# A fused transformer block on one core: fewer bands of the depthwise convolution on TensorE, more of its products by DMA, and a newly computed order

## The chip, the core and the metric

The kernel runs on one core of a Trainium2 chip. The core has five engines with a queue of instructions each: PE (TensorE, matmuls; its weight loads are listed as PEld), DVE (VectorE), ACT (ScalarE), POOL (GpSimd) and SP (SyncE, which here only issues transfers), and 16 DMA engines that move data. An engine runs its queue in order; between engines, semaphores tell when a result is there. The metric is the device time of one execution in microseconds (us). All data are float32.

## The reference

The input is x of shape 16 x 128 x 96 x 96 (images, channels, rows, columns). One block of an image-restoration transformer is computed: layer norm over the channels, attention between the channels within 8 heads, a residual sum, a second layer norm, a feed-forward part, and a residual sum.

```python
x = x + attn_out                      # attention of layernorm(x, ln1)
xn2 = layernorm(x, ln2)               # over the 128 channels
h1 = einsum('bchw,oc->bohw', xn2, w_in)          # 128 -> 512 channels
h2 = depthwise 3x3 convolution of h1, zero padding, w_dw   # each of 512 channels by itself
h3 = gelu(h2)
x = x + einsum('bchw,oc->bohw', h3, w_out)       # 512 -> 128 channels
```

The change concerns the depthwise convolution, h1 to h2: for each of the 512 channels nine products with shifted images, added up.

## The kernel before

**Tiling.** Channels lie on the 128 partitions. An image is cut into 8 bands of 12 rows (`BR`, 1152 pixels), 128 bands in all (`NG`), and a band into three strips of 4 rows (384 pixels). The 512 hidden channels are four blocks of 128 (n = 0 to 3). So the convolution consists of 128 x 4 pieces (g, n), a band and a block of channels.

**Two ways to compute a piece.** `conv_job` does it with all engines: PE makes h1 of the band from the normalized image (`hidden`, L907), ACT copies it out of PE's accumulators into an SBUF image with a border (`kept`, L912), and then the nine products are shared out. All weights are divided by that of the middle tap (`UNIT`), which then needs no multiplication. DVE computes the first tap with the middle tap added (L925), and each further tap as one instruction, multiply by the channel's weight and add in place (`tap`, L931). Some taps are not computed by DVE: ACT multiplies the shifted image by its weight into a product buffer `pr` (`product`, L920), and a DMA that accumulates adds it up (`add_products`, L941, issued by POOL): the second product of the piece into the first one's buffer (pr<-pr), and the first one's buffer into h3 when DVE is done with its taps (h<-pr). Two taps go this way in every piece (`DMA_TAPS`), and a third one where `third` (L948) holds. Such a piece has one more `pr<-pr` transfer and one tap fewer on DVE. Then ACT applies GELU in place (L945).

`by_matmuls` does a piece of block 3 on PE alone: it takes the composition of w_in and one tap's weights as nine 128 x 128 matrices (`comp`), and accumulates nine matmuls on each strip of the normalized image, 27 for the band (L991); every float32 matmul shows as two passes. GELU then reads the accumulators (L1001). Such a piece needs no h1, no taps, no products and no DMA. `by_pe(g)` (L1041) says which bands have it: counted from the end, k = NG - 1 - g, those of `PE_LAST` among the last eight, and of the others those with k % `PE_OF` in `PE_BANDS`.

`ffn_out` (L1009) multiplies h3 by w_out, four matmuls on each strip (L1018), DVE adds the result to x (L1025), and SP stores the band (L1029). The two norms of every image run beside the convolution of other bands: transposes on PE (L615, L720), statistics on DVE (L622), variance and power on POOL (L629, L633), scaling on ACT (L669, L673), and a Gram matrix on PE (L683). x comes in by SP (L552), and is added to the attention's result by an accumulating DMA that POOL issues (L584).

**The order.** No engine's queue is written by hand. Every step is an `op` of a `Plan` with an engine, a cost in ns, a place, and the buffers that it reads and writes. `Plan.order` (L104) plays the whole program through with these costs: a free engine takes, of the steps whose inputs are ready and whose buffers are free, the one with the lowest place; the steps are then issued in the order of their planned starts. A place is the number of the job plus the kind's offset from the table `AT`. The costs come from `t_mm`, `t_dve`, `t_act`, `t_copy` (L375 and after) and from constants: `T_ADD` for the time that an accumulating transfer occupies the DMA engines, `T_MOVE` for a plain one. Buffers are counted in the plan too: five product buffers (`PR_BUFS`), ten h3 buffers, six and two of x, three of transposed strips, four accumulator banks for matmul results.

Of the kernel before, what the change touches and what calls it, by code (L numbers as in the profile page):

```python
# [17 lines left out]
UR = 4  # L18
BR = 12
PE_CHUNK = 3  # L20
PE_BANDS = (0,)
PE_OF = 2
PE_LAST = (0, 1, 2, 4, 5, 7)
TINY = 1e-20
UNIT_MIN = 1e-18
# [2 lines left out]
FIRST_TAP, THIRD_TAP = 7, 1  # L28
TOP_FIRST, TOP_THIRD = 7, 8
END_FIRST, END_THIRD = 1, 0  # L30
THIRD, THIRD_OF, THIRD_CHUNK = (0, 1, 2), 3, 1
PART, Z_PARTS = 24, 6
QT, QB = 4, 1
H_BANKS = 4
X1_BUFS, XB_BUFS, PR_BUFS, H3_BUFS, ZT_BUFS = 2, 6, 5, 10, 3
IN_TURN = ("tr", "h3", "pr", "xb", "x1")
AT = dict(
    load_w=-0.7, weights=56.25, zeros=-91.75, load_a=-171.6, forth_a=-13.8, stats_a=-13.35, variance_a=472.9,
    power_a=393.55, scaled_a=100.7, gram=-0.95, back_a=-54.2, place_a=177.7, attention=-168.4, mix=-35.75,
    residual=220.5, mixed=-116.4, add_x=-284.15, forth_b=-10.05, stats_b=-175.75, variance_b=89.4,  # L40
    power_b=-306.7, shift_b=-89.65, scaled_b=147.3, back_b=-5.05, place_b=36.3, halo=257.25, hidden=4.1,
    kept=-157.6, products=108.95, add_last=-2.05, tap=5.45, add_first=-115.65, gelu=233, conv=3.9, conv_gelu=5,
    out=7.4, add=-85.8, store=312.6, mix_0=-83.1, residual_0=398.2, mixed_0=-274.7, add_x_0=-395.85,
    gram_0=56.85, forth_a_0=-241.65, forth_b_0=-12.45, stats_a_0=-45.05, stats_b_0=-53.25, scaled_a_0=38.7,
    scaled_b_0=263.2, back_a_0=-243.25, back_b_0=-126.9, place_a_0=-340.95, place_b_0=-9.4, shift_b_0=-42.6,
    late=7.15,
)
STEP = dict(scaled=0.3, hidden=0.1, products=0.5, tap=0.166, conv=1.6, conv_tap=0.03, out=0.8, out_part=0.05)
SLACK = 300
# [3 lines left out]
T_START = 2300  # L53
T_VARIANCE = 420
T_POWER = 1000
T_ADD, T_MOVE = 3060, 1640


class Plan:
# [14 lines left out]
    def op(self, engine, ns, place, work, reads, writes, result, own=None, dma=0, two=False):  # L74

        k = len(self.ops)  # L80
        needs = {}
        for t in reads:
            if t in self.writer:
                needs[self.writer[t]] = True
        for t in writes:
            if t in self.writer:
                needs[self.writer[t]] = True
            for r in self.readers.get(t, ()):
                needs[r] = True
        for t in reads:  # L90
            self.readers.setdefault(t, []).append(k)
        new = []
        for t in writes:
            self.writer[t], self.readers[t] = k, []
            if t[0] in self.free and t[:2] not in self.users and t[:2] not in new:
                new.append(t[:2])
        for t in {t[:2]: None for t in (*reads, *writes)}:
            if t[0] in self.free:
                self.users.setdefault(t, []).append(k)
                needs[self.users[t][0]] = True  # L100
        needs.pop(k, None)
        self.ops.append((engine, ns, place, work, list(needs), new, result, own or result, dma, two))
# [111 lines left out]
def tile_restormer_block(  # L214
# [30 lines left out]
    UT = UR * W  # L245
    TPU = UT // P
# [26 lines left out]
    ones = const.tile([P, 1], F32, name="ones")  # L273
# [79 lines left out]
    def x_unit(of, i, u):  # L353
# [5 lines left out]
        tr=2, bk=1, h=H_BANKS, g=1, batch=4, zT=ZT_BUFS, x1=X1_BUFS, xb=XB_BUFS, pr=PR_BUFS, h3=H3_BUFS  # L359
# [3 lines left out]
    def at(kind, place, i=1):  # L363
        return place + AT[kind if i else kind + "_0"]

    def bank(key, n=4 * P):

        return banks[plan.slot["h", key]][:, :n]
# [4 lines left out]


    def t_mm(n):  # L375
        return 2 * max(110, 0.84 * n)

    def t_dve(n):
        return 100 + 1.067 * n

    def t_act(n, scalars=0):
        return 95 + 93 * scalars + 0.832 * n
# [1 line left out]
    def t_copy(n):  # L384
        return 40 + 0.832 * n

    def pe(ns, p, f, r, w):
        op("PE", ns, p, f, r, w, ns + 200 + SLACK, ns)
# [150 lines left out]
    def x_key(i, b, second):  # L539

        return "xb" if second or i == 0 and b < XB_BUFS else "x1"
# [14 lines left out]
    def norm(i, second, place_of):  # L556

        name = f"{'b' if second else 'a'}{i}"
        ab = "_b" if second else "_a"
        zTs = {}  # L560

        def xtok(u):
            return (x_key(i, u // UPB, second), (i, u // UPB), u % UPB)
# [34 lines left out]
        def pixels(s, m):  # L598
# [8 lines left out]
            def forth(q):  # L607
                if early:
                    d["pT", q] = bank((name, q)).rearrange("p (t c) -> p t c", c=P)
                else:  # L610
                    d["pT", q] = p_tr.tile([P, QT, P], F32, tag="tr", name=f"pT_{name}_{q}")
                for k in range(QT):
                    b, j = divmod(q * QT + k, TPB)
                    xt = (xbs if x_key(i, b, second) == "xb" else x1s)[i, b]
                    nc.tensor.transpose(d["pT", q][:, k, :], xt[:, j * P : (j + 1) * P], ident)  # L615
# [62 lines left out]
            def gram(q):  # L678
                if q == 0:
                    grams[i] = p_g.tile([P, 4 * P], F32, tag="g", name=f"g_{i}")  # L680
                for k in range(QT):
                    zt = zTs[q][:, k, :]
                    nc.tensor.matmul(  # L683
                        grams[i][:, : P + 1], lhsT=zt[:, :P], rhs=zt,
                        start=(q == 0 and k == 0), stop=(q == NU * TPU // QT - 1 and k == QT - 1),
                    )

            trs, bt = [(key_, (name, q)) for q in qs], ("batch", (name, m))
            for q, tr in zip(qs, trs):
                units = {t // TPU: None for t in range(q * QT, (q + 1) * QT)}  # L690
                pe(110 * QT, at("forth" + ab, s, i), lambda q=q: forth(q), [xtok(u) for u in units], [tr])
            for j in range(QB * QT // 2):
                dve(341, at("stats" + ab, s, i), lambda j=j: stats(j), [trs[2 * j // QT]], [bt])
            op("POOL", T_VARIANCE, at("variance" + ab, s), variance, [], [bt], T_VARIANCE + 33 + SLACK + 200)
# [3 lines left out]
            for h, (q, tr) in enumerate(zip(qs, trs)):  # L698
                zt, sh = zt_of(q), s + STEP["scaled"] * h
                if by_dve:  # L700
                    if apart and q % 2 == 0:
                        both = [(*zt_of(k), j) for k in (q, q + 1) for j in range(2)]
                        op("POOL", 200, at("zeros", sh), lambda q=q: zT(q), [], both, 300)
                    dve(by_dve * 240, at("scaled" + ab, sh, i), lambda q=q: also_scaled(q), [tr, bt], [(*zt, 0)])
                act((QT - by_dve) * (343 if second else 250), at("scaled" + ab, sh, i), lambda q=q: scaled(q), [tr, bt], [(*zt, 1)])
                if not second:
                    pe(QT * 220, at("gram", sh, i), lambda q=q: gram(q), [(*zt, 0), (*zt, 1), ("w", "ones")], [("g", i)])

        def zt_of(q):
            return ("h3", ("zT", q // 2), q % 2) if i == 0 and not second else ("zT", (name, q))  # L710

        def channels(s, u):

            d = {}

            def back():
                d["pB"] = p_bk.tile([P, UT], F32, tag="bk", name=f"pB_{name}_{u}")
                for j in range(TPU):
                    q, k = divmod(u * TPU + j, QT)
                    nc.tensor.transpose(d["pB"][:, j * P : (j + 1) * P], zTs[q][:, k, :P], ident)  # L720

            def place():
                if second:
                    nc.scalar.activation(interior(i, u), rows(d["pB"]), AF.Identity, bias=b2)
                else:
                    nc.scalar.copy(interior(i, u), rows(d["pB"]))

            def place_row(k, r, row):
                to = window(xns[k], r, 1, 1)
                nc.scalar.activation(to, rows(d["pB"])[:, row : row + 1, :], AF.Identity, bias=b2)  # L730

            copies = []
            if second and u % UPP == 0 and u > 0:
                copies.append((part_of(i, u * UR - 1)[0], PART + 1, 0, UPP))
            if second and u % UPP == UPP - 1 and u < NU - 1:
                copies.append((part_of(i, (u + 1) * UR)[0], 0, UR - 1, -1))

            pb = ("bk", (name, u))
            quads = {(u * TPU + j) // QT: None for j in range(TPU)}
            pe(110 * TPU, at("back" + ab, s, i), back, [(*zt_of(q), k) for q in quads for k in range(2)], [pb])  # L740
            act(t_act(UT, 1) - 43 if second else t_copy(UT), at("place" + ab, s, i), place, [pb, ("w", "shift")] if second else [pb], [z_unit(i, u)])
            for k, r, row, of in copies:
                act(225, at("place" + ab, s, i), lambda k=k, r=r, row=row: place_row(k, r, row), [pb, ("w", "shift")], [("z", k, of)])
# [7 lines left out]
        u = 0  # L751
# [135 lines left out]
    def conv_job(j, g, n):  # L887

        i, b = divmod(g, NB)
# [55 lines left out]
            nc.scalar.activation(h3, h3, AF.Gelu)  # L945

        last = j == len(jobs) - 1
        third = n == THIRD_CHUNK and g % THIRD_OF in THIRD  # L948
        ahead, also = (TOP_FIRST, TOP_THIRD) if b == 0 else (END_FIRST, END_THIRD) if b == NB - 1 else (FIRST_TAP, THIRD_TAP)
        dma_taps = () if last else (*DMA_TAPS, also) if third else DMA_TAPS  # L950
        left = [ahead, *(t for t in range(9) if t not in (ahead, UNIT, *dma_taps))]
# [89 lines left out]
    def by_pe(g):  # L1041
        k = NG - 1 - g
        return k in PE_LAST if k < NB else k % PE_OF in PE_BANDS

# [58 lines left out]
```

## Time and profile before

| | |
|---|---|
| three runs | 4160.88, 4160.81, 4159.0 us; median 4160.81 |
| the profiled execution | 4157.91 us, of which its span (first to last instruction) is 4156.2 |
| granted PE clock, mean | 0.998 of full speed |
| PE busy | 4116.1 us, 99% |
| DVE busy | 4023.1 us, 97% |
| ACT busy | 3673.4 us, 88% |
| POOL busy | 2466.3 us, 59% |
| DMA engines, queue of POOL and queue of SP | 83.4% and 10.2% of the span |

Busy time is the time in which an engine has at least one instruction running. Instructions of one engine overlap a little, so the durations of a group add up to more than the engine's time. In the lists of groups a line reads: source line, engine, operation, written tile <- read tiles, shape, count | busy time of the group in us, mean duration of one in ns | idle time of the engine just before them, and what ended it. A list of stretches has, for each window in us from the span's start, the busy time of every engine with its number of instructions, the granted PE clock, the DMA engines' mean busy share and what they moved. The share can be slightly over 1, since two packets on one DMA engine can overlap in the records.

### The profile page before, as it was taken

What the parts mean: (1) busy time and instruction counts of PE and PEld (TensorE: products, weight loads), DVE (VectorE), ACT (ScalarE), POOL (GpSimd) and SP (SyncE); (2) the same over time, 40 slices, a digit from 0 to 9 for tenths busy, and PEclk for the clock granted to TensorE, in tenths of its full rate; (3) what the DMA queues carried; (4) which work ended last, traced back from release to release, by engine and by line L of the source; (5) the groups of instructions that cost most, each with busy time, mean ns of one, the idle gap of its engine ahead of it and who ended that gap; (6) DMA issues with size and microseconds to landing.
All of it is one profiled execution on the core that took longest, in us unless ns stands there. A gap on an engine that the chain in (4) does not pass through costs nothing.

```text
span 4156.2 us, 52372 instructions
## 1 busy us (share of the span) xinstructions
PE 4116.1 (99%) x17457; PEld 2679.0 (64%) x17457; DVE 4023.1 (97%) x4676; ACT 3673.4 (88%) x6971; POOL 2466.3 (59%) x2347
## 2 busy tenths in 40 slices
PE   8999999999999999999999999999999999999999
PEld 7666666666666666666666666666666666666565
DVE  7999999999999999999999999999999999999998
ACT  5999998999989888998999989888898998989885
POOL 4667565565656657566465656656557565665442
PEclk9999999999999999999999999999999999999999
DMA  3999999999999989999999999999999999999997
GB/s 94 195 203 212 195 214 203 208 206 197 212 202 208 201 189 212 204 208 203 195 217 189 210 213 193 213 196 202 207 197 211 204 206 196 191 211 190 193 195 171
DMA packets 203934, 827.63 MB, mean 199 GB/s; under 512 B 23568, under 2 KB 24976, under 8 KB 203664
## 3 DMA queue, kind: packets, MB, share of 16 engines
q0 software_dynamic: 164160, 672.47, 83.4%
q1 hardware_dynamic: 38256, 151.73, 10.2%
q8 instruction: 138, 2.26, 0.2%
q14 instruction: 132, 1.08, 0.1%
q10 hardware_dynamic: 1248, 0.09, 0.0%
HBM read 148.26 MB, written 75.50 MB: 54 GB/s over the span
## 4 chain that ended last, share of the span: by engine, by line
PE 84%; ACT 7%; DVE 5%; DMA 2%; issue 1%; POOL 1%; POOLq 0%; ACTq 0%; DVEq 0%
PE h L991 22%; PE h L1018 21%; PE h L907 18%; PE g L683 5%; PE h L572 5%; DVE h L931 3%; PE pB_a L720 3%; PE pT_b L615 3%; PE pT_a L615 2%; PE pB_b L720 2%; ACT pr L920 2%; DMA pr<-pr 1%; ACT zT L673 1%; DMA h<-pr 1%; ACT h L912 1%
## 5 line engine op out<-in xcount | busy, mean ns | idle before, releaser
L931 DVE SCALAR_TENSOR_TENSOR h<-h,ratio,h 128x1140 f32<-128x1140 f32 (+2 forms) x2104 | 2856.9, 1379 | 5.3
L920 ACT ACTIVATE pr<-h,ratio 128x1152 f32<-128x1152 f32 x1018 | 1310.4, 1295 | 69.1 <-DMA h<-pr 41.1
L991 PE MATMUL h<-xn,comp 128*128 128x380 f32 (+1 forms) x3564 | 1261.9, 481 | 4.3 <-ACT h L912 3.9
L1018 PE MATMUL h<-h,woutT 128*128 128x384 f32 x3072 | 1134.1, 488 | 6.2 <-ACT h L945 4.9
L907 PE MATMUL h<-xn,winT 128*128 128x384 f32 (+1 forms) x2676 | 1045.3, 494 | 4.3 <-ACT h L912 2.9
L991 PEld LDWEIGHTS h<-xn,comp 128*128 128x128 f32 x3564 | 645.9, 189 | 380.4 <-issue 8.2
L941 POOL DMA_DIRECT2D pr<-pr x573 | 557.9, 988 | 507.5 <-ACT pr L920 332.2
L912 ACT COPY h<-h 128x384 f32<-128x384 f32 (+1 forms) x1338 | 652.1, 513 | 187.4 <-PE h L907 175.5
L1018 PEld LDWEIGHTS h<-h,woutT 128*128 128x128 f32 x3072 | 555.3, 190 | 335.6 <-ACT h L945 17.9
L941 POOL DMA_DIRECT2D h<-pr x445 | 428.8, 966 | 469.2 <-PE h L907 66.6
L907 PEld LDWEIGHTS h<-xn,winT 128*128 128x128 f32 x2676 | 481.6, 190 | 292.5 <-issue 42.2
L925 DVE SCALAR_TENSOR_TENSOR h<-h,ratio 128x1152 f32<-128x1152 f32 x446 | 625.8, 1408 | 19.7 <-ACT h L912 10.8
L945 ACT ACTIVATE h<-h 128x1152 f32<-128x1152 f32 x448 | 537.3, 1203 | 12.3 <-DMA h<-pr 9.2
L633 POOL TENSOR_TENSOR rstd_a<-ve_a,mhalf 128x4 f32<-128x4 f32 x288 | 513.8, 1784 | 12.3 <-POOL ve_a L629 0.2
L633 POOL TENSOR_TENSOR rstd_b<-ve_b,mhalf 128x4 f32<-128x4 f32 x288 | 496.0, 1723 | 12.2
L629 POOL TENSOR_SCALAR ve_b<-st_b 128x4 f32<-128x4 f32 x288 | 290.1, 1007 | 269.0 <-DVE st_b L622 259.5
L629 POOL TENSOR_SCALAR ve_a<-st_a 128x4 f32<-128x4 f32 x288 | 305.4, 1061 | 241.7 <-DVE st_a L622 213.8
L673 ACT ACTIVATE zT<-pT_b,nb_b,rstd_b 128x128 f32<-128x128 f32 x1132 | 433.9, 497 | 13.7 <-DVE nb_b L637 12.6
L669 ACT ACTIVATE zT<-pT_a,rstd_a 128x128 f32<-128x128 f32 x1080 | 314.6, 403 | 11.5 <-POOL rstd_a L633 6.7
L683 PEld LDWEIGHTS g<-zT 128*128 128x128 f32 x2304 | 292.4, 191 | 36.7 <-issue 1.7
L683 PE MATMUL g<-zT 128*128 128x129 f32 x2304 | 304.9, 275 | 0.0
L572 PE MATMUL h<-xn,mwT 128*128 128x384 f32 x768 | 287.1, 489 | 5.2 <-ACT h L912 4.1
(171 smaller groups left out, 3568.0 us busy)
## 6 DMA issues: line engine op xcount, KB each, us to landing
pr<-pr POOLq DMA_DIRECT2D x573, 576.0 KB, 7.5
h<-pr POOLq DMA_DIRECT2D x445, 576.0 KB, 7.1
x<-in_x_dram SPq DMA_DIRECT2D x128, 576.0 KB, 6.8
out_dram<-x SPq DMA_DIRECT2D x127, 576.0 KB, 6.0
x<-in_x_dram POOLq DMA_DIRECT2D x122, 576.0 KB, 7.1
out_dram<-x SPq DMA_DIRECT2D x3, 192.0 KB, 1.9
weights<-in_L_conv_w_in_dram SPq DMA_DIRECT2D x1, 256.0 KB, 3.0
weights<-in_L_conv_w_out_dram SPq DMA_DIRECT2D x1, 256.0 KB, 3.2
```

Of the source, the lines that this page charges most:

```text
L629: nc.gpsimd.tensor_scalar(ve, d["mv"][:, :, 2], 1.0 / C, EPS, ALU.mult, ALU.add)
L633: nc.gpsimd.tensor_tensor(rstd, d["ve"], mhalf, ALU.pow)
L683: nc.tensor.matmul(grams[i][:, : P + 1], lhsT=zt[:, :P], rhs=zt, start=(q == 0 and k == 0), stop=(q == NU * TPU // QT - 1 and k == QT - 1),)
L907: nc.tensor.matmul(rows(ph), lhsT=winT[:, n, :], rhs=window(xn, r0 + r, e - r, 1), start=True, stop=True)
L912: nc.scalar.copy(window(h1_, r, e - r, 1), rows(d.pop(("ph", r))))
L920: nc.scalar.activation(to, shifted(t), AF.Copy, scale=ratio[:, n, t : t + 1])
L925: nc.vector.scalar_tensor_tensor(h3, shifted(t), ratio[:, n, t : t + 1], shifted(UNIT), ALU.mult, ALU.add)
L931: nc.vector.scalar_tensor_tensor(to, shifted(t)[:, lo:hi, cut], ratio[:, n, t : t + 1], to, ALU.mult, ALU.add)
L941: nc.gpsimd.dma_start(out=to, in_=d["pr", t], accum_op=ALU.add)
L945: nc.scalar.activation(h3, h3, AF.Gelu)
L991: nc.tensor.matmul(d["pc"][:, lo:hi, cut], lhsT=comp[:, t, :], rhs=window(xn, r0 + dy, UR, dx)[:, lo:hi, cut], start=(t == order[0]), stop ...
L1018: nc.tensor.matmul(rows(d["po"]), lhsT=woutT[:, n, :], rhs=h3s[g, n][:, s * UR : (s + 1) * UR, :], start=(k == 0), stop=(k == NCH - 1),)
```

## The change

- `PE_OF` goes from 2 to 15 and `PE_BANDS` from (0,) to the seven even numbers up to 12: of the bands before the last eight, 56 instead of 60 have block 3 on PE; with `PE_LAST`, which stays, 62 instead of 66. In the four others, block 3 becomes a `conv_job`.
- The third product, which block 1 had in every band, stays there, and block 2 has it in every fourth band as well (32 bands).
- The order is computed anew: all offsets in `AT` but a few have other values, matmuls are costed at 0.849 ns a column instead of 0.84, small DVE instructions a little cheaper, transposes at 112 ns, the Gram matmuls at 228, an accumulating transfer at 2960 ns instead of 3060 and a plain one at 1450 instead of 1640. What each step computes is the same.

```diff
-PE_BANDS = (0,)
-PE_OF = 2
+PE_BANDS = (0, 2, 4, 6, 8, 10, 12)
+PE_OF = 15
 PE_LAST = (0, 1, 2, 4, 5, 7)
...
-THIRD, THIRD_OF, THIRD_CHUNK = (0, 1, 2), 3, 1
+THIRDS = ((1, 1, (0,)), (2, 4, (0,)))
...
-    kept=-157.6, products=108.95, add_last=-2.05, tap=5.45, add_first=-115.65, gelu=233, conv=3.9, conv_gelu=5,
...
+    kept=-117.6, products=83.4, add_last=-10.7, tap=4.7, add_first=-163.25, gelu=198.35, conv=4.05,
+    conv_gelu=4.55, out=7.5, add=-70.3, store=341.25, mix_0=-83.1, residual_0=410.6, mixed_0=-181.35,
...
-T_ADD, T_MOVE = 3060, 1640
+T_ADD, T_MOVE = 2960, 1450
...
     def t_mm(n):
-        return 2 * max(110, 0.84 * n)
+        return 2 * max(111, 0.849 * n)
 
     def t_dve(n):
-        return 100 + 1.067 * n
+        return 100 + 1.067 * n if n > 2 * UT else 67 + 1.05 * n
...
-                pe(110 * QT, at("forth" + ab, s, i), lambda q=q: forth(q), [xtok(u) for u in units], [tr])
+                pe(112 * QT, at("forth" + ab, s, i), lambda q=q: forth(q), [xtok(u) for u in units], [tr])
...
-                    pe(QT * 220, at("gram", sh, i), lambda q=q: gram(q), [(*zt, 0), (*zt, 1), ("w", "ones")], [("g", i)])
+                    pe(QT * 228, at("gram", sh, i), lambda q=q: gram(q), [(*zt, 0), (*zt, 1), ("w", "ones")], [("g", i)])
...
-            pe(110 * TPU, at("back" + ab, s, i), back, [(*zt_of(q), k) for q in quads for k in range(2)], [pb])
+            pe(112 * TPU, at("back" + ab, s, i), back, [(*zt_of(q), k) for q in quads for k in range(2)], [pb])
...
-        third = n == THIRD_CHUNK and g % THIRD_OF in THIRD
+        third = any(n == c and g % of in gs for c, of, gs in THIRDS)
```

More of the change, by code (lines that the diff above doesn't have):

```diff
@@ L37 @@
 AT = dict(
[L38 to L41, printed above, removed]
-    kept=-157.6, products=108.95, add_last=-2.05, tap=5.45, add_first=-115.65, gelu=233, conv=3.9, conv_gelu=5,
[L43 to L46, printed above, removed]
+    load_w=-24.8, weights=-72.2, zeros=-112.8, load_a=-134.95, forth_a=-11.75, stats_a=-4.7, variance_a=556.2,
+    power_a=373.25, scaled_a=76, gram=0.85, back_a=-23.65, place_a=140.75, attention=-136.4, mix=-66.95,
+    residual=243.55, mixed=-111.55, add_x=-252.6, forth_b=-9.2, stats_b=-145.8, variance_b=69.55,
+    power_b=-306.2, shift_b=-65.1, scaled_b=179.65, back_b=-34.45, place_b=42.6, halo=216, hidden=4.1,
+    kept=-117.6, products=83.4, add_last=-10.7, tap=4.7, add_first=-163.25, gelu=198.35, conv=4.05,
+    conv_gelu=4.55, out=7.5, add=-70.3, store=341.25, mix_0=-83.1, residual_0=410.6, mixed_0=-181.35,
+    add_x_0=-276.4, gram_0=29.95, forth_a_0=-213.2, forth_b_0=-10.4, stats_a_0=14.15, stats_b_0=-46.4,
+    scaled_a_0=55.15, scaled_b_0=280.05, back_a_0=-221.4, back_b_0=-203.5, place_a_0=-257.3, place_b_0=-14.8,
+    shift_b_0=-100.3, late=-36.95,
 )
```

## The prediction

> **What bounds the kernel now.** I read the page's busy totals and slices first, then the costliest groups, then stretches of 104 us, and last the waits of single engines.
>
> ```profile
> span 4156.2 us, 52372 instructions
> PE 4116.1 (99%) x17457; PEld 2679.0 (64%) x17457; DVE 4023.1 (97%) x4676; ACT 3673.4 (88%) x6971; POOL 2466.3 (59%) x2347
> q0 software_dynamic: 164160, 672.47, 83.4%
> q1 hardware_dynamic: 38256, 151.73, 10.2%
> PE 84%; ACT 7%; DVE 5%; DMA 2%; issue 1%; POOL 1%; POOLq 0%; ACTq 0%; DVEq 0%
> L931 DVE SCALAR_TENSOR_TENSOR h<-h,ratio,h 128x1140 f32<-128x1140 f32 (+2 forms) x2104 | 2856.9, 1379 | 5.3
> L920 ACT ACTIVATE pr<-h,ratio 128x1152 f32<-128x1152 f32 x1018 | 1310.4, 1295 | 69.1 <-DMA h<-pr 41.1
> L991 PE MATMUL h<-xn,comp 128*128 128x380 f32 (+1 forms) x3564 | 1261.9, 481 | 4.3 <-ACT h L912 3.9
> L941 POOL DMA_DIRECT2D pr<-pr x573 | 557.9, 988 | 507.5 <-ACT pr L920 332.2
> L941 POOL DMA_DIRECT2D h<-pr x445 | 428.8, 966 | 469.2 <-PE h L907 66.6
> L945 ACT ACTIVATE h<-h 128x1152 f32<-128x1152 f32 x448 | 537.3, 1203 | 12.3 <-DMA h<-pr 9.2
> ```
>
> TensorE (PE) is idle for 40.1 us of the span and carries 84% of the chain that ended last: it is the bound. VectorE (DVE) is idle for 133.1 us; the DMA engines are busy 94% (queues 0 and 1 together). So three resources are nearly full, and a saving on one is worth only what the next allows. The duration of a matmul pass (481 ns) is not its price, since passes overlap; the pace is in the chain in order of time (start, length, what): 18 passes in 5.77 us, 0.321 us each.
>
> ```profile
> 567.82 5.77 PE h L991 x18
> ```
>
> The stretches (length, busy time of PE, PEld, DVE, ACT, POOL, granted clock, DMA share, GB/s) tell how the engines fill together:
>
> ```profile
> 0.00:104.00 104.00, 92.79 (x596) 76.02 (x597) 73.62 (x204) 57.83 (x151) 45.97 (x107) 0.97 0.32 94
> 1040.00:1144.00 104.00, 104.00 (x465) 69.69 (x464) 103.19 (x120) 94.35 (x183) 71.40 (x64) 1.00 1.00 212
> 1456.00:1560.00 104.00, 102.48 (x423) 64.87 (x421) 95.44 (x116) 92.65 (x174) 52.38 (x52) 1.00 0.90 189
> 2080.00:2184.00 104.00, 104.00 (x457) 69.11 (x456) 103.60 (x118) 94.87 (x182) 72.03 (x65) 1.00 1.02 215
> 104.00:4056.00 3952.00, 3926.68 (x16556) 2545.78 (x16555) 3862.81 (x4399) 3559.92 (x6742) 2400.47 (x2217) 1.00 0.96 203
> 4056.00:4160.00 104.00, 96.64 (x308) 57.22 (x306) 86.65 (x75) 55.69 (x80) 19.85 (x23) 0.99 0.76 164
> ```
>
> A stretch with DMA at 1.00 to 1.02 can have PE at 104.00 and DVE above 103: full DMA engines alone do not stall the rest. DVE's idle time is 30.4 us in the first stretch, 89.2 in the middle and 13.5 at the end. What DVE and ACT wait for, from the waits of each engine (total, times, longest):
>
> ```profile
> DVE x L1025 <- PE h L1018: 24.9, 34, 2.9
> DVE st_b L622 <- PE pT_b L615: 20.4, 28, 6.1
> ACT pr L920 <- DMA h<-pr: 41.1, 45, 4.9
> ACT pr L920 <- DMA pr<-pr: 24.4, 23, 2.3
> ```
>
> DVE waits mostly for PE, which the change relieves. ACT waits 65.5 us for product buffers to come free from adding DMAs, which the change loads more.
>
> **The change, part by part.** Counts are from the instruction order of the two built kernels.
>
> *Conv on PE in 62 bands, not 66.* Removed: 108 matmuls of L991, two passes each: 105 of 380 or 384 columns at 0.321 us and three of 285 or 288 columns at 0.24 (by width): 68.9 us. Added: 12 hidden matmuls (L907; eight of 480 columns at 0.40 us a pass, three of 384, one of 288): 8.8 us. PE, on the path, sheds 60.1 us.
>
> *The four bands' block 3 on DVE.* By the rows of each shape (1408, 1406, 1393, 1293 and about 1300 ns): four first taps and twenty others come in (+33.4 us); *the third product in block 2 of every fourth band* takes 32 taps out (-44.6). The order's counts by shape (+4, -13, -2, +2, +1) net eight taps fewer, **-11.5 us of DVE**.
>
> *ACT.* 40 products at 1.295 us, 12 copies L912 at 0.513, four GELUs at 1.203, less 12 of L1001 at 0.514: +56.6 us, to 3730 us, some 91% of the new span. It lies in ACT's idle time; if that cover goes, the copies that feed DVE are late. The 16 activation-table loads stay 16.
>
> *POOL.* 40 more issues of L941 at 0.98 us, 39 us on an engine that is 59% busy. An add that waits for its product holds up the variance and power steps queued behind it (332.2 us of such waits over 573 issues, 0.58 us each, so 23 us more); ACT's scaling (L669, L673) waits for those steps, and PE's transposes back for that. Hidden by POOL's 1690 us of idle time unless it falls on a late batch: 0 to 23 us, taken as 2.
>
> A rule that speaks against this part: the Trainium skill, "GPSIMD Engine Reference", in its first table, has GpSimd's SBUF interfaces shared with VectorE and in contention with VectorE instructions that read two SBUF inputs, which the taps are. The row of L941 has issues of 850 ns at least, 905 in the median and 2587 at most; were all 40 held as the longest was, the rule would make 104 us of POOL time out of 39, still under its idle time.
>
> *DMA.* 83.4% of the span over 1140 accumulating transfers (573 + 445 + 122) is 3.04 us each: 40 more are **+122 us** of DMA time, the largest addition. The middle stretch holds 0.96 x 3952 = 3794 us; it becomes 3916. At a mean share s in the middle, the span is 104 + 3916/s + 100: 4120 at s = 1.00, 4043 at 1.02 (the fullest stretch above), 4160 at 0.99, 4200 at 0.98.
>
> The Trainium skill, "DMA: Bandwidth & Descriptors", section on the anatomy of a DMA on the GpSimd path, gives 2.0 us plus bytes over 436 GB/s: by my estimate 3.4 us for one of these 576 KB transfers, of which 1.35 us is data. The trace has 7.1 to 7.5 us to landing and 3.04 us of engine time. By the page the 40 would cost 54 us of DMA and never bind; the measurement decides.
>
> *The new order.* All priorities (AT) and five planner times change, so every instruction may move on every queue, SP's loads and stores included. The trace cannot price it. From below: all of PE's 40.1 us idle goes, -40. From above: DVE's middle idle time stays as it is although DVE has less slack. DVE's floor is 4011.6 busy + 30.4 + 13.5 at the ends + 0.6 us per stretch (the mean of the two with DMA at 1.00 and 1.02: 0.8 and 0.4) x 38 = 4078; the other 66 us of middle idle on top make 4145, that is +49 over PE's floor of 4096. I take +17: most of the 66 is DVE waiting for the PE that is now relieved, but DMA at a share of 1.00 asks for 4120. The ends count as unchanged.
>
> **Sum.** The profiled execution took 4157.9 us (span 4156.2 and 1.7 around it; 2.9 under the median of 4160.8). 4157.9 - 60.1 + 2 + 17 = 4116.8; rounded to **4116 us**, 1.1% less than the median.
>
> **Rivals.**
> 1. *DMA queue becomes the bound: slower.* Adds land late, the five product buffers come free late, ACT stands at a product (L920) with the copies L912 queued behind it, and DVE and PE starve. For: 0.96 before, 1.00 wanted; stretches at 0.90 to 0.92 exist, with DVE at 95 us. Against: the stretches at 1.00 and 1.02 cost PE nothing. It decides below a mean share of 0.99; at 0.98 the time is 4200 + 2 = 4202 us.
> 2. *DVE becomes the bound.* Its 66 us of middle idle stay: 4145 + 2 = **4147 us**, barely faster. For: DVE's floor of 4078 is 18 us under PE's 4096, where it was 66 under (4090 against 4156). Against: the waits named are on PE.
> 3. *The better times also remove half of PE's idle time.* 4157.9 - 60.1 - 20 = **4078 us**. For: the new costs are nearer the trace (0.326 us for 384 columns). Against: much of PE's idle time is at the start (11.2 us in the first stretch), and DVE would then stand at its floor of 4078 without a single late tap.
> That the change does not do what it says is excluded by the counts.
>
> **How the numbers follow.** Forecast (4096 to 4135) 0.55; rival 3, 0.10; rival 2 (4135 to 4155), 0.15; rival 1, 0.20. The measurement can tell about 0.2%, 8 us. Faster (under 4152): 0.55 + 0.10 + 0.10 of rival 2 = 0.75. Same: 0.05 of rival 2 and 0.02 of rival 1, 0.07. Slower: the remaining 0.18. The range 4086 to 4166 leaves out most of rival 3 and the worse half of rival 1, together under 0.2.
>
> **What would show it.** PE busy near 4056 us, L991 x3348; DVE busy near 4012; L941 x1058 and q0 near 87%; middle DMA share about 1.00 with PE's stretches still 103 to 104. If ACT's wait at L920 for DMAs grows well beyond 65 us and DVE's wait for L912 with it, rival 1 holds; if DVE has the larger part of the chain, rival 2. I am wrong if transfers at a mean share of 1.00 land much later than 7.5 us, or if the new start costs more than 11.2 us of PE.

## The result, and the profile after

The changed kernel takes 4183.93 us in the median of six runs (4176.61 to 4193.44), against 4159.69 us for the kernel before in the runs beside them: a time ratio of 1.0062, with a 95% interval of 1.0047 to 1.0077. It is **slower by 0.6%**, about 24 us, where 44 us less had been forecast. Its profiled execution took 4179.1 us, of which 4177.4 are the span.

The page of the kernel after, busy totals, DMA queues, chain and costliest groups:

```profile
span 4177.4 us, 52059 instructions
PE 4090.7 (98%) x17265; PEld 2638.3 (63%) x17265; DVE 4015.9 (96%) x4668; ACT 3708.0 (89%) x7015; POOL 2485.1 (59%) x2387
q0 software_dynamic: 169920, 696.07, 85.6%
q1 hardware_dynamic: 38256, 151.73, 9.9%
PE 51%; DMA 15%; DVE 12%; ACT 11%; issue 3%; POOL 2%; POOLq 0%; ACTq 0%
L920 ACT ACTIVATE pr<-h,ratio 128x1152 f32<-128x1152 f32 x1058 | 1363.2, 1302 | 176.6 <-DMA h<-pr 87.4
L991 PE MATMUL h<-xn,comp 128*128 128x380 f32 (+2 forms) x3348 | 1176.2, 482 | 0.2 <-ACT h L1001 0.2
L925 DVE SCALAR_TENSOR_TENSOR h<-h,ratio 128x1152 f32<-128x1152 f32 x450 | 635.5, 1416 | 47.5 <-ACT h L912 32.5
```

The counts are those of the change (L991 x3348, L920 x1058). What was one chain of PE instructions (84%) is now a mixture: PE 51%, and DMA, DVE and ACT have 38% between them. PE is idle for 87 us instead of 40, DVE for 162 instead of 133, though both have less work: they wait for something else. The waits of ACT and DVE name it (total, times, longest); the last line is the first taps' group of the kernel before:

```profile
ACT pr L920 <- DMA h<-pr: 87.4, 79, 3.7
ACT pr L920 <- DMA pr<-pr: 85.5, 92, 3.7
ACT h L945 <- DMA h<-pr: 28.3, 18, 6.1
DVE h L925 <- ACT h L912: 32.5, 35, 3.1
```

```profile
L925 DVE SCALAR_TENSOR_TENSOR h<-h,ratio 128x1152 f32<-128x1152 f32 x446 | 625.8, 1408 | 19.7 <-ACT h L912 10.8
```

ACT stands 172.9 us before a product, because no product buffer is free until a transfer has landed; before it was 65.5. Behind the product in ACT's queue stand the copies L912 and the scaling, and DVE's wait for L912 grows from 10.8 to 32.5 us. PE's matmuls of all kinds now wait for ACT in many small pieces (63.1 us in 95 waits, where it was 25.7 us in 36). The DMA issues (count, size, median us to landing), first two of the kernel before, then after, and the stretches of the middle and of one bad and two full 104 us:

```profile
pr<-pr POOLq DMA_DIRECT2D x573, 576.0 KB, 7.5
h<-pr POOLq DMA_DIRECT2D x445, 576.0 KB, 7.1
```

```profile
pr<-pr POOLq DMA_DIRECT2D x609, 576.0 KB, 7.7
h<-pr POOLq DMA_DIRECT2D x449, 576.0 KB, 7.3
104.00:4056.00 3952.00, 3881.49 (x16298) 2493.42 (x16297) 3836.60 (x4368) 3577.44 (x6760) 2410.08 (x2246) 1.00 0.98 208
312.00:416.00 104.00, 102.62 (x462) 68.21 (x461) 103.99 (x121) 96.54 (x188) 71.09 (x65) 1.00 1.01 222
416.00:520.00 104.00, 99.23 (x419) 63.68 (x419) 96.88 (x120) 93.50 (x183) 61.91 (x58) 0.98 0.91 191
1352.00:1456.00 104.00, 99.60 (x442) 65.24 (x441) 102.51 (x115) 94.55 (x183) 74.72 (x64) 1.00 1.02 218
```

Transfers take only 0.2 us longer to land than before, in the median. The middle share is 0.98. Now PE loses time also where DMA is full: 99.60 busy at a share of 1.02, where before a stretch at the same share had 104.00. So a full stretch was no proof that full DMA engines cost nothing.

### The profile page after: what moved, and what is told of

It reads as the page before. It is cut to its first block, busy times and chain, and to the rows that moved or that the text cites. A ratio compares the mean times of both kernels' runs of the same rounds, so it can differ in the third digit from the quotient of the medians.

```text
span 4177.4 us, 52059 instructions
## 1 busy us (share of the span) xinstructions
PE 4090.7 (98%) x17265; PEld 2638.3 (63%) x17265; DVE 4015.9 (96%) x4668; ACT 3708.0 (89%) x7015; POOL 2485.1 (59%) x2387
## 4 chain that ended last, share of the span: by engine, by line
PE 51%; DMA 15%; DVE 12%; ACT 11%; issue 3%; POOL 2%; POOLq 0%; ACTq 0%
PE h L1018 14%; PE h L991 14%; PE h L907 11%; DMA pr<-pr 8%; DVE h L931 8%; DMA h<-pr 6%; ACT pr L920 3%; PE g L683 3%; PE h L572 3%; DVE h L925 2%; PE pB_a L720 2%; PE pT_b L615 2%; ACT zT L673 2%; PE pB_b L720 1%; ACT h L912 1%
## 5 line engine op out<-in xcount | busy, mean ns | idle before, releaser
L931 DVE SCALAR_TENSOR_TENSOR h<-h,ratio,h 128x1140 f32<-128x1140 f32 (+3 forms) x2092 | 2861.5, 1386 | 7.7
L920 ACT ACTIVATE pr<-h,ratio 128x1152 f32<-128x1152 f32 x1058 | 1363.2, 1302 | 176.6 <-DMA h<-pr 87.4
L991 PE MATMUL h<-xn,comp 128*128 128x380 f32 (+2 forms) x3348 | 1176.2, 482 | 0.2 <-ACT h L1001 0.2
L1018 PE MATMUL h<-h,woutT 128*128 128x384 f32 x3072 | 1116.2, 487 | 14.6 <-ACT h L912 7.4
L907 PE MATMUL h<-xn,winT 128*128 128x384 f32 (+2 forms) x2700 | 1051.5, 495 | 6.2 <-ACT h L912 4.3
L941 POOL DMA_DIRECT2D pr<-pr x609 | 587.0, 970 | 542.8 <-ACT pr L920 303.8
L991 PEld LDWEIGHTS h<-xn,comp 128*128 128x128 f32 x3348 | 606.9, 189 | 352.5 <-issue 9.1
L912 ACT COPY h<-h 128x384 f32<-128x384 f32 (+2 forms) x1350 | 669.5, 529 | 106.6 <-PE h L907 96.7
L941 POOL DMA_DIRECT2D h<-pr x449 | 430.1, 960 | 539.3 <-DMA pr<-pr 93.2
L925 DVE SCALAR_TENSOR_TENSOR h<-h,ratio 128x1152 f32<-128x1152 f32 x450 | 635.5, 1416 | 47.5 <-ACT h L912 32.5
L945 ACT ACTIVATE h<-h 128x1152 f32<-128x1152 f32 x452 | 544.9, 1210 | 32.8 <-DMA h<-pr 28.3
L633 POOL TENSOR_TENSOR rstd_b<-ve_b,mhalf 128x4 f32<-128x4 f32 x288 | 491.4, 1707 | 10.8
L629 POOL TENSOR_SCALAR ve_a<-st_a 128x4 f32<-128x4 f32 x288 | 323.5, 1124 | 191.7 <-DVE st_a L622 175.7
```

The costliest lines, as they stand in the source:

```text
L629: nc.gpsimd.tensor_scalar(ve, d["mv"][:, :, 2], 1.0 / C, EPS, ALU.mult, ALU.add)
L633: nc.gpsimd.tensor_tensor(rstd, d["ve"], mhalf, ALU.pow)
L907: nc.tensor.matmul(rows(ph), lhsT=winT[:, n, :], rhs=window(xn, r0 + r, e - r, 1), start=True, stop=True)
L912: nc.scalar.copy(window(h1_, r, e - r, 1), rows(d.pop(("ph", r))))
L920: nc.scalar.activation(to, shifted(t), AF.Copy, scale=ratio[:, n, t : t + 1])
L925: nc.vector.scalar_tensor_tensor(h3, shifted(t), ratio[:, n, t : t + 1], shifted(UNIT), ALU.mult, ALU.add)
```

## The experiments

Four theories stood to be told apart: **A1**, five product buffers are too few; **A2**, the throughput of the DMA engines binds; **B**, the new order is worse by itself; **C**, PE and DVE are now so nearly equal in load that they stall each other. After the first four runs came **D**: the order counts on transfers landing earlier than they do. All ratios are to the kernel before, run on the same chip in turn, with 95% intervals. The runs lie on several chips, so differences in us between them are good to a few us.

### Half of every product transfer

```diff
-            nc.gpsimd.dma_start(out=to, in_=d["pr", t], accum_op=ALU.add)
+            nc.gpsimd.dma_start(out=to[:, : BR // 2], in_=d["pr", t][:, : BR // 2], accum_op=ALU.add)
```

> The kernel after, but every accumulating product transfer moves only the first half of the band (six of twelve rows), so the sum is left out for the other half. Order, engines' work and buffers stay; DMA work falls by some 1600 us. A1 and A2: products' buffers come free sooner, the wait at L920 nearly vanishes, 4090 to 4125. B and C: PE and DVE have the same work in the same order, 4165 to 4185.

Measured: 4103.12 us, ratio 0.9870 (0.9857 to 0.9884), 81 us less than the kernel after. From its page and the waits of ACT:

```profile
PE 4058.8 (99%) x17265; PEld 2642.8 (64%) x17265; DVE 4005.3 (98%) x4668; ACT 3709.9 (90%) x7015; POOL 2516.4 (61%) x2387
PE 59%; DVE 23%; ACT 8%; issue 3%; DMA 1%; POOL 0%; DVEq 0%; POOLq 0%; ACTq 0%
ACT pr L920 <- DMA h<-pr: 2.8, 4, 1.2
ACT pr L920 <- DMA pr<-pr: 2.6, 4, 1.4
```

The same instructions in the same order on PE, DVE and ACT, and with DMA out of the way they reach what was forecast for them: PE 99% busy with 4059 us (forecast 4056), DVE 98% with 4005 (4012). C falls as the main cause, and so does an order that would be bad for PE and DVE themselves. (Half of each product transfer still moves: the middle DMA share is 0.64.)

The same edit on the kernel before:

> The kernel before, with accumulating product transfers over half of the rows, as in the run of the kernel after that took 4103 us. With DMA out of the way only PE's work is left of the difference: if the 60 us of PE are right, 4150 to 4160, that is 45 to 60 us more than the changed kernel so treated; if also before was held up by DMA, 4120 to 4145.

Measured: 4143.85 us, 0.9967 (0.9954 to 0.9979), 15 us less than before. Its chain:

```profile
PE 88%; ACT 6%; DVE 3%; issue 1%; DMA 1%; POOL 1%; POOLq 0%; DVEq 0%; ACTq 0%
```

So the time divides: with product transfers halved in both, the change is worth 4143.85 - 4103.12 = 41 us; the other half of the transfers costs the kernel before 15 us and the kernel after 81, which is 66 more. 41 - 66 = -25 is the measured loss of 24, as it must be: the sum shares the loss out between work and DMA, and is no test of it.

### One twelfth of the product transfers, or most of the stores

In the kernel after, each product transfer moves eleven of the twelve rows:

```diff
-            nc.gpsimd.dma_start(out=to, in_=d["pr", t], accum_op=ALU.add)
+            nc.gpsimd.dma_start(out=to[:, : BR - 1], in_=d["pr", t][:, : BR - 1], accum_op=ALU.add)
```

> The kernel after, with each accumulating product transfer over eleven of the twelve rows (the twelfth row's product is not added). Same order; a transfer gets some 8% shorter, about 250 us of DMA time in all. Theory D (the order was computed with 2960 and 1450 ns for transfers where before it was 3060 and 1640, so real transfers land later than the order counts on, and a small relief suffices): most of the 81 us that the half transfers gave come back, 4105 to 4135. Theory A1 (the number of product buffers): a smaller part, 4150 to 4170, since buffers are held little shorter.

Measured: 4128.71 us, 0.9926 (0.9913 to 0.9940). With the product transfers whole and seven eighths of each store left out:

```diff
-            at_ = slice(b * BR * W + k * UT, b * BR * W + (k + n) * UT)
-            nc.sync.dma_start(out=ov[i, :, at_], in_=xbs[i, b][:, k * UT : (k + n) * UT])
+            at_ = slice(b * BR * W + k * UT, b * BR * W + k * UT + n * UT // 8)
+            nc.sync.dma_start(out=ov[i, :, at_], in_=xbs[i, b][:, k * UT : k * UT + n * UT // 8])
```

> The kernel after, with each band's store to DRAM cut to an eighth of its columns (the rest of the output is left out). Same order; product transfers and buffers untouched; some 170 us of plain transfers leave the DMA engines. If the throughput of the DMA engines as a whole binds (A2, D): 4120 to 4150. If only the handling of product buffers does (A1): 4170 to 4185.

Measured: 4139.00 us, 0.9952 (0.9939 to 0.9964). The queue of each that got shorter (packets, MB, share of the span), first the one with eleven rows, then the one with small stores:

```profile
span 4124.4 us, 52494 instructions
q0 software_dynamic: 169920, 644.07, 81.9%
```

```profile
span 4139.8 us, 52055 instructions
q1 hardware_dynamic: 38256, 85.67, 6.3%
```

The first took 3576 - 3378 = 198 us of DMA time from its queue and won 55 us; the second 414 - 261 = 153 us and won 45. The other queue took some more time in each (7 and 17 us), so both queues together lost 191 and 136 us. That is about 0.3 us won for each us (0.29 and 0.33), whichever transfers are relieved, also those that never touch a product buffer. Waits for a store come to some 7 us in all in the kernel after, none longer than 3.0, so buffers that a store sets free are not what the second run won by. The engines' throughput is what matters (A2); a lack of product buffers alone (A1) had 4170 to 4185 us for the second. The price is not constant: the first 191 us gave 55 of the 81 us that halving gave, the next 1220 or so gave the other 26.

The eleven rows in the kernel before:

> The kernel before with accumulating product transfers over eleven of the twelve rows. The kernel after won 55 us by this. D: before has room already, and with half of each transfer it won only 15 us, so 4144 to 4154. If relief of DMA helps any kernel alike: 4100 to 4125.

Measured: 4146.81 us, 0.9974 (0.9963 to 0.9985): 12 us for 196 us of DMA time (78.9% of 4145.0 against 83.4% of 4156.2), 0.06 for each.

```profile
q0 software_dynamic: 164160, 622.44, 78.9%
```

The same transfer time costs the kernel before a fifth of what it costs the kernel after. The two differ in load and in order, so this pair does not tell which of them raised the price.

### A sixth product buffer

```diff
-    prp = ctx.enter_context(tc.tile_pool(name="prp", bufs=PR_BUFS))
+    prp = ctx.enter_context(tc.tile_pool(name="prp", bufs=PR_BUFS + 1))
...
-    woutT = const.tile([P, NCH, P], F32, name="woutT")
-    comp = const.tile([P, 9, P], F32, name="comp")
+    woutT = const.tile([P, 2, P], F32, name="woutT")
+    comp = const.tile([P, 4, P], F32, name="comp")
```

> The kernel after with a sixth physical product buffer; the planned order stays the same instruction for instruction. To make room, the convolution on TensorE uses four tap matrices for nine and the output product two for four, so its result is another; counts and sizes of all instructions of the steady state stay. Theory A1 (too few product buffers: ScalarE's wait at L920 for DMAs grew from 65 to 173 us): that wait falls under 65 us and the time to 4100 to 4130. Theory A2 (the DMA engines' throughput binds, buffers only show it): wait moves elsewhere, 4165 to 4185. Theory B (the new order by itself is worse) and C (PE and DVE are so nearly equal in load that they stall each other): 4170 to 4190.

Measured: 4145.59 us, 0.9969 (0.9956 to 0.9981), 38 us less than after. Its waits of ACT:

```profile
ACT h L945 <- DMA h<-pr: 63.3, 44, 6.1
ACT pr L920 <- DMA pr<-pr: 4.1, 6, 1.4
```

The wait before the product is gone (172.9 to 4.1), but only 38 of the 81 us came back: GELU (L945) now waits 63.3 us for the last transfer of its piece, 28.3 before. A1 is half right: a buffer more takes ACT out of the queue, and the late transfer is felt one step on.

> The kernel before with a sixth physical product buffer in the same order (with four tap matrices for nine and two output matrices for four, which changes the result, to make room). A1 and D: its wait at L920 for DMAs is 65 us and mostly covered, so within 0.3% of before, 4145 to 4165; if buffers bind both kernels alike, 4110 to 4130.

Measured: 4151.21 us, 0.9981 (0.9972 to 0.9989): 7 us. The sixth buffer is worth five times as much to the kernel that loads DMA more.

### Order and division apart

The order of the new offsets and costs with the old division:

```diff
-PE_BANDS = (0, 2, 4, 6, 8, 10, 12)
-PE_OF = 15
+PE_BANDS = (0,)
+PE_OF = 2
...
-THIRDS = ((1, 1, (0,)), (2, 4, (0,)))
+THIRD, THIRD_OF, THIRD_CHUNK = (0, 1, 2), 3, 1
...
-        third = any(n == c and g % of in gs for c, of, gs in THIRDS)
+        third = n == THIRD_CHUNK and g % THIRD_OF in THIRD
```

> The old division of the work (66 bands on TensorE, third product in block 1 alone) in an order computed with the new offsets and costs. B: 4175 to 4200, slower than before. A and C: within 0.3% of before, 4145 to 4170.

Measured: 4195.89 us, 1.0092 (1.0078 to 1.0106). The reverse edit on the kernel before, the new division under the old offsets and costs:

> The new division of the work (62 bands on TensorE, 32 more third products) in an order computed with the old offsets and costs. B: the 60 us that TensorE sheds show, 4100 to 4125. A and C: the stalls come with the division, 4165 to 4195.

Measured: 4241.09 us, 1.0203 (1.0189 to 1.0216). Each half alone is slower than both together. The first lies in the range of B, the second above every range that was given (its granted clock was 0.989 to 0.992, where the other runs had 0.996 or more). Both were long before they met the chip: played again off the chip with the kernel's own offsets and costs, the plan (`Plan.order`) starts its last step at 4148.9 and 4200.6 us, while the same offsets and costs with the division that they were found for give 4104.8 (the kernel after) and 4109.3 (before). So the offsets belong to their division; the two runs do not weigh order against load, and neither B nor A and C is decided by them.

### The same division with room for the transfers

The cost of a transfer in the planner was lowered by the change. For each accumulating transfer of a trace I took its time from issue to landing, less the time that the order had counted for the same transfer. Before, 15% of them came later than counted; after, 34%. So the order was computed three times more for the new division with more room for transfers, with offsets looked for anew each time; the steps, their sizes and the bytes are those of the kernel after.

```diff
-T_ADD, T_MOVE = 2960, 1450
+T_ADD, T_MOVE = 3000, 1500
```

> The new division of the work as in the kernel after, the same steps and DMA bytes, in an order computed with slightly longer transfers (3000 and 1500 ns instead of 2960 and 1450) and offsets looked for anew under these costs. Theory D (the order counts on transfers landing earlier than they do): fewer adds land later than the order counts on, 4140 to 4165. Theory A2 (the DMA load itself, whatever the order): 4175 to 4195.

Measured: 4158.30 us, 0.9998 (0.9989 to 1.0006).

```diff
-T_ADD, T_MOVE = 2960, 1450
+T_ADD, T_MOVE = 3030, 1550
```

> As before it, with 3030 and 1550 ns and offsets of its own. D: the more room, the less waiting, 4130 to 4160, if the order is otherwise as good. A2: 4175 to 4195.

Measured: 4155.93 us, 0.9991 (0.9983 to 1.0000).

```diff
-        op("POOL", 950, p, f, r, w, 1400 + SLACK, dma=T_ADD)
+        op("POOL", 950, p, f, r, w, 2100 + SLACK, dma=T_ADD)
```

> The new division, in an order computed with 2960 and 1450 ns, but with every accumulating transfer counted as landed 700 ns later than the kernel after counts it; offsets looked for anew. This gives the transfers room in latency, not in DMA time. D, if latency is what matters: 4130 to 4160. If it is the DMA engines' throughput that the order overrates: 4165 to 4190, no better than after.

Measured: 4140.96 us, 0.9954 (0.9941 to 0.9968), **faster than both kernels**. Its share of late transfers is 17%, and its waits at L920 are 111 us:

```profile
PE 4082.0 (98%) x17265; PEld 2645.9 (64%) x17265; DVE 4016.0 (97%) x4668; ACT 3704.2 (89%) x7015; POOL 2527.8 (61%) x2387
ACT pr L920 <- DMA h<-pr: 59.6, 59, 3.0
ACT pr L920 <- DMA pr<-pr: 51.7, 55, 4.2
```

Looking for offsets anew could have done this by itself. Two runs tell: the costs of the kernel after untouched, new offsets alone; and a middle dose of room (1800 + SLACK).

> The new division, with exactly the costs of the kernel after (2960 and 1450 ns, no added latency), and only the offsets looked for anew, with the same effort as for the kernels with more room. If the room for transfers is what made those faster (theory D): no gain, 4175 to 4195. If it was only the new search (theory S): 4140 to 4165 here as well.

Measured: 4160.87 us, 1.0015 (1.0006 to 1.0023). In this kernel the lines stand one higher, L919 for L920:

```profile
ACT pr L919 <- DMA h<-pr: 93.9, 79, 3.7
ACT pr L919 <- DMA pr<-pr: 83.1, 89, 3.8
```

> As the kernel whose transfers count as landed 700 ns later (4141 us), but with 400 ns. D: between after and that one, 4145 to 4170. S: as good as or better than it, 4130 to 4145.

Measured: 4143.46 us, 0.9965 (0.9952 to 0.9979).

The table has the six kernels of the new division side by side: the share of transfers that came later than counted, the start of the last step in the plan when it is played again, the measured median, and what the chip took beyond the plan.

| kernel | late | plan, us | measured, us | beyond the plan, us |
|---|---|---|---|---|
| after | 34% | 4104.8 | 4183.9 | 79 |
| new offsets alone | 34% | 4097.9 | 4160.9 | 63 |
| 3000 and 1500 ns | 25% | 4109.0 | 4158.3 | 49 |
| 3030 and 1550 ns | 19% | 4118.8 | 4155.9 | 37 |
| 400 ns later | 26% | 4113.4 | 4143.5 | 30 |
| 700 ns later | 17% | 4118.7 | 4141.0 | 22 |

New offsets alone win 20 us over the kernel after by the ratios (1.0062 to 1.0015), 7 of them already in the plan, the rest for a reason that these runs do not show; they leave the stall as it was (177 us before the product) and do not reach the kernel before. D had forecast no gain there (4175 to 4195), so it is not the whole account. Room in latency wins 21 and 25 us more by the ratios (to 0.9965 and 0.9954), room in the length of transfers 7 and 10. The offsets of each kernel were looked for once, and one search moves the time by as much as the room does, so luck of the search stays a rival. Against it stand the plans: those with 400 and 700 ns of room are 16 and 21 us longer than that of the new offsets alone, and the chip keeps to them more closely. That fits D, and is not proof of it; several searches at equal costs would tell. Neither the share of late transfers nor the wait before the product is by itself a measure of the time: the kernel with 400 ns has 26% late and waits 153 us, and is faster than the one with 3030 ns, which has 19% and 131 us.

## Why the prediction was wrong, point by point

- *PE sheds 60 us, DVE 11.5, ACT gains 57, POOL 39.* With product transfers halved in both kernels, PE's busy time falls by 51 us (4110.0 to 4058.8), nine less than counted, and DVE's by 16 (4021.2 to 4005.3). ACT gained 35, since its durations overlap; POOL 19. In time, the work is worth 41 us, not 60: PE is idle for 44 us where the kernel before, so treated, has 34. The chain of the kernel after then has 23% of DVE, that of the kernel before 3%, which fits the second rival's DVE with less slack, but no run shows it by itself. Activation-table loads are 32 in both traces; the 16 of the prediction are those before a GELU.
- *DMA gains 122 us.* The queue of the accumulating transfers gained 110 (3466 to 3576), both queues together 99, since SP's took 10 less for the same bytes. Right in kind, some 23 us too large.
- *The new order, +17, bounded by +49.* This is the term that failed, and the step behind it is the reading that full DMA engines do not stall the rest. By the sum the term would have had to be some +84: 4157.9 - 60.1 + 2 + 84 = 4184. The bounds were drawn from DVE's idle time alone; what DMA cost was argued away by two stretches at a share of 1.00 and 1.02 in which PE stood full. Such stretches are picked moments: the kernel after has one at 1.02 with PE at 99.60. In place of no cost, halving the transfers gave 81 us back after and 15 before: 66 us more of stall, which with the 19 us that the work fell short make up the miss (66 + 19 - 17 = 68, from 44 forecast as won to 24 lost). By the runs with a little less DMA work the price was about 0.3 us per us.
- *"The trace cannot price it."* The plans could have warned: by its own costs the new order starts its last step at 4104.8 us, the old one at 4109.3. That is 4.5 us apart and not 44, though the costs differ (matmuls are about 1% dearer in the new one), so it is no clean comparison.
- *Rival 1, the slower one, chance 0.20.* It named the chain that the profile shows: product buffers late, ACT at L920, L912 behind it, DVE and PE starved. Its threshold, slower below a mean share of 0.99, came true with 0.98, but the share is DMA work over time and falls whenever the time grows: it restates the loss and does not cause it. Its time of 4202 us was 18 too much. With the 99 us of DMA time that came instead of 122 its sum gives 104 + 3893/0.98 + 100 + 2 = 4178; since the share is known to two digits, some 20 us either way, that is no test. Of the two signs of being wrong that the prediction gave, neither showed what happened: transfers did not land much later than 7.5 us in the median, and PE's idle time in the first 104 us grew from 11.2 to 12.7 us only. More transfers came later than the order had counted, 34% for 15%.
- *Measured times in the planner as an argument for the change.* No run shows what the matmuls' costs gave by themselves. For transfers, the lower figures left less room for their spread, and the kernels with more room were faster than the one with new offsets alone.
- *The GpSimd rule.* The median issue of L941 stayed at 904 and 907 ns (905 and 913 before), though POOL issues 40 more beside DVE's taps: the added issues show no added contention. Whether both kernels have some, no run shows.

## What to carry to other kernels

Where an order is fixed in advance and an engine runs in order, the cost of a transfer in the planner had better leave room for its spread: orders that counted on a landing 0.4 and 0.7 us later had longer plans, and ran the same work 21 and 25 us faster than new offsets alone (one search for offsets each). Before work is moved to DMA engines that are 96% busy, price it at the margin: take a known amount of transfer time away and see what it gives. In the kernel before that was 0.06 us per us; in the kernel after, with some 100 us more of load and another order, about 0.3, so a price found before a change need not hold behind it. Play the plan of the new order before the chip does: it showed both mixed kernels to be slow. A stretch of the profile in which a resource is full and nobody waits tells of that order alone.

## What the runs showed of the hardware that was not expected

A higher load hardly changed the transfers themselves: 7.5 and 7.1 us to landing became 7.7 and 7.3 while the middle share went from 0.96 to 0.98. The Trainium skill, "Perfetto Trace Analysis", section "Identifying the Most-Contended Engine", advises judging DMA by the use of HBM, not by the occupancy of its 16 engines, and then finding which DMA resource binds. Here HBM moved 54 GB/s over the span in both kernels, and all transfers together 199 and 204 GB/s, since most of them run from SBUF to SBUF; what the engines' busy share of 0.96 and more told, the use of HBM did not: 191 us of their time less, with the same HBM bytes, made the kernel after 55 us faster. The share does not rank kernels either: the one with 700 ns of room has 0.99 in the middle, more than the 0.98 of the kernel after, and is 43 us faster.
